# A long planned pause of TensorE takes several products with zeros instead of one

## Chip, cores, metric

The kernel runs on one core of a Trainium2 chip. The metric is the device time of one execution in microseconds (us). The core's engines are TensorE (PE; its weight loads are PEld), VectorE (DVE), ScalarE (ACT), GpSimd (POOL) and SyncE (SP, which issues the DMAs here). Every program is one launch, and the inputs are fixed.

## What is computed

Two pre-norm layers act on x of 8 sequences × 512 tokens × 128 features, all in float32:

```
x = x + linear_attention(layernorm(x))   # 16 heads × 64; elu(.)+1 features of q and k; sums over the sequence;
                                         # per feature q * kv / (q * ksum + eps); output projection; gelu
x = x + fp4_ffn(layernorm(x))            # inputs and weights rounded to blocks of FP4; 128 -> 352 -> 128, silu gate
x = x + causal_attention(layernorm(x))   # 16 heads × 8, softmax over a lower triangle
x = x + experts(layernorm(x))            # rms norm, 8 low-rank adapters on one shared 128 -> 512 -> 128 FFN,
                                         # the best 2 of 8 per token, weighted
```

## The kernel before, in words

Each sequence b (0 to 7) is one tile of 128 partitions × 4 × 128. It passes through eight kinds of work, the lanes: loads, norm, linear, out, fp4, attention, routing, experts. While one sequence is in its attention, others are in linear, fp4 or experts, so that the first 200 us are mostly linear and fp4 work, the middle has all of them, and the end has only the experts of the last sequence.

The kernel text doesn't issue instructions in the order in which it is written. It records steps: each call through `nc.<engine>` becomes a `Step` with its engine, its needs (steps that must be done) and a planned cost from a formula in `cost`. `Plan.ordered` (line 249) then plays the steps through with these costs and with a rank for each step from the table `TURNS`, and so gives every step a planned start and end and the program order of each engine. `Plan.issue` (line 397) writes the instructions in that order. On the chip each engine takes its own instructions strictly in program order and waits on semaphores for the others; the planned times play no part any more. Because all calls come out of `issue`, the profile shows nearly everything under one line, L407, and groups are told apart by the names of their tiles.

The names that the later sections use: `ahead` (one bank of PSUM), `pair` (two) and `mid` (one) are where products land. `wq`, `wk`, `wv` and `xnT` are the projections of the linear attention; each product of 512 columns is followed by `relu` and `exp` on ACT and a combination on DVE (`kf`, `qf`), then `z` (ACT), `r` (POOL, then the DVE reciprocals of some 1.7 us) and `qf` (POOL). `wk_o` is the weighted output matrix; four products of it make half of the linear attention's output, which goes to `y`. `xf`, `qa`, `sc`, `h`, `hq`, `wT` belong to fp4, `qkT`, `pr`, `va` and `mask_q` to the causal attention. `tT`, `a_sb`, `w_sb`, `um`, `b_sb`, `act` belong to the experts; `ohr`, `top`, `s4 routing` and `pb` to the routing. A float32 product of 512 columns appears in the profile as two MATMUL records.

`Plan.kept_warm` (line 365) runs over the finished order. For each step of TensorE it looks at the planned pause before it (`gap`) and at the work that TensorE had in the last 3.413 us of the plan (`worked`). Where work is lacking and `want` is over 0.2 us, it puts one extra step on TensorE's queue at the start of the pause: a product of up to 512 columns, `plan.warmer(n)` (line 907), whose moving operand is the tile `zeros` and whose weights are the identity, accumulated into `mid`. It adds zero to what is there. Its planned cost is 1.7 ns per column. In the profile these are the records `mid<-zeros,ident`; here they are called warmers. A warmer is left out where the planned time lies between TensorE's last write of `mid` and the last read of it (`read`), so that a reader of `mid` doesn't wait for it. Since the class `Clock` is not in use for durations (`MODEL` is false), the plan reckons with one speed of TensorE.

## Time and profile before

| | |
|---|---|
| time, median of 3 runs | 1132.38 us (1130.52 to 1133.14) |
| the profiled execution's own time | 1131.95 us |
| its span, first to last instruction | 1130.1 us |
| mean granted clock of TensorE | 0.982 |
| PE busy | 1040.2 us, 92% of the span |
| DVE / ACT / POOL busy | 73% / 56% / 55% |
| records of `mid<-zeros,ident` | 88 |

The span is 1.85 us shorter than the execution's time. Busy time of PE counts records that overlap by their modelled ends, so its share says where PE has work, and not how well it is used. In the rows of the timeline the first number is the start, the second the duration of a merged group, `xN` the number of its records, and the bracket the idle time of the engine before it with what ended it. In a windows view the pairs are busy time and number of records of each engine, then the mean granted clock, the share of the DMA engines and their GB/s. "Half clock" below is a granted clock of 0.50.

### The profile page before, as it was taken

To read this page: it belongs to the slowest core of one execution; us is meant where nothing else is said; L and a number is where in the kernel's file an instruction comes from. 1 tells how busy PE (TensorE), PEld (TensorE's weight loads), DVE (VectorE), ACT (ScalarE), POOL (GpSimd) and SP (SyncE) were. 2 spreads that over 40 slices of the span, in tenths; PEclk is the share of its full clock that TensorE was granted. 3 is DMA by queue.
4 is the path that set the end of the run, shared out by engine and by line. 5 is a ranking of instruction groups with operands and counts; after the bars stand their busy time and mean duration, and the time that the engine had idled before them with its cause. 6 is when DMAs were issued, how large, how long until landed. Compare 5 with 4: busy or idle time off the path is not lost.

```text
span 1130.1 us, 15043 instructions
## 1 busy us (share of the span) xinstructions
PE 1040.2 (92%) x5025; PEld 488.0 (43%) x5025; DVE 830.3 (73%) x1868; ACT 630.8 (56%) x1084; POOL 624.3 (55%) x669
## 2 busy tenths in 40 slices
PE   6667788998899999999998999999999999999998
PEld 2223333344344444444543444454454445445454
DVE  6868879897888967758788968788667765556543
ACT  5756787678786644644578555764443443344311
POOL 6647846676676466237635755467644533441534
PEclk9879989999999999999999999999999999999999
DMA  8000030001101020111012000210002102001000
GB/s 235 1 1 0 1 111 1 21 20 56 39 20 30 10 94 20 58 72 35 26 39 94 19 21 20 95 30 19 20 7 98 39 20 104 21 20 30 1 10 9
DMA packets 30572, 44.31 MB, mean 39 GB/s; under 512 B 4192, under 2 KB 18464, under 8 KB 30496
## 3 DMA queue, kind: packets, MB, share of 16 engines
q1 hardware_dynamic: 30496, 43.37, 11.9%
q8 instruction: 39, 0.64, 0.2%
q14 instruction: 37, 0.30, 0.1%
HBM read 23.95 MB, written 18.87 MB: 38 GB/s over the span
## 4 chain that ended last, share of the span: by engine, by line
PE 57%; DVE 15%; ACT 6%; issue 2%; POOL 1%; DMA 0%; POOLq 0%; DVEq 0%; ACTq 0%
PE ahead L407 31%; PE pair L407 19%; PE mid L407 7%; ACT pr L407 2%; DVE r L407 2%; DVE mx L407 2%; DVE h L407 1%; DVE sc L407 1%; ACT qf L407 1%; DVE s4 routing L407 1%; DVE qf L407 1%; DVE act L407 1%; ACT z L407 1%; DVE kf L407 1%; DVE oh L407 1%
## 5 line engine op out<-in xcount | busy, mean ns | idle before, releaser
L407 ACT ACTIVATE pr<-pair 128x1024 f32<-128x1024 f32 (+1 forms) x192 | 166.7, 879 | 149.2 <-PE pair L407 129.1
L407 DVE TENSOR_REDUCE mx<-pair 128x4 f32<-128x512 f32 (+2 forms) x192 | 198.5, 1041 | 68.4 <-PE pair L407 57.7
L407 POOL TENSOR_SCALAR_AFFINE_SELECT pr<-pr 128x256 f32<-128x256 f32 (+1 forms) x192 | 92.8, 485 | 176.4 <-ACT pr L407 175.6
L407 PE MATMUL pair<-qkT 32*128 32x128 f32 (+7 forms) x1024 | 172.3, 387 | 9.4 <-ACT pr L407 2.7
L407 PEld LDWEIGHTS pair<-qkT 32*128 32x128 f32 (+1 forms) x1024 | 84.4, 183 | 181.8 <-ACT pr L407 52.0
L407 POOL TENSOR_TENSOR act<-act,tw 128x512 f32<-128x512 f32 x64 | 81.3, 1272 | 88.8 <-DVE act L407 80.6
L407 PE MATMUL ahead<-um,b_sb 128*128 128x512 f32 x240 | 122.2, 607 | 0.0
L407 DVE RECIPROCAL r<-r 128x256 f32<-128x256 f32 x64 | 110.3, 1736 | 14.9 <-POOL r L407 14.8
L407 DVE SCALAR_TENSOR_TENSOR act<-act,ahead 128x512 f32<-128x512 f32 x120 | 81.9, 684 | 51.4 <-ACT act L407 38.0
L407 POOL TENSOR_TENSOR qa<-qa,qa 128x704 f32<-128x704 f32 (+4 forms) x60 | 81.2, 1354 | 35.1 <-DVE qa L407 26.2
L407 POOL TENSOR_TENSOR qf<-qf,r 128x512 f32<-128x512 f32 x64 | 80.5, 1278 | 34.5 <-DVE r L407 27.8
L407 PE MATMUL mid<-pr,va 128*10 128x512 f32 (+3 forms) x1024 | 93.3, 435 | 0.0
L407 POOL TENSOR_TENSOR qf<-qf,z 128x512 f32<-128x512 f32 x64 | 80.3, 1270 | 0.0
L407 ACT ACTIVATE act<-ahead 128x512 f32<-128x512 f32 x60 | 35.8, 597 | 72.0 <-PE ahead L407 71.9
L407 PE MATMUL ahead<-act,a_sb 128*128 128x512 f32 x128 | 65.2, 619 | 0.0
L407 POOL TENSOR_TENSOR r<-z,z 128x512 f32<-128x512 f32 x32 | 40.9, 1278 | 41.6 <-ACT z L407 39.3
L407 PE MATMUL ahead<-tT,w_sb 128*128 128x512 f32 x120 | 63.3, 609 | 0.0
L407 ACT ACTIVATE ahead<-ahead,bqkv_sb 128x512 f32<-128x512 f32 x96 | 63.0, 656 | 0.0
L407 PE MATMUL pair<-mask_q,ident 128*128 128x128 bf16 (+1 forms) x384 | 61.6, 242 | 0.0
L407 PE MATMUL ahead<-xnT,wk 128*128 128x512 f32 x100 | 56.7, 650 | 4.8 <-DVE kf L407 2.1
L407 PEld LDWEIGHTS ahead<-um,b_sb 128*128 128x128 f32 x240 | 40.7, 190 | 36.1 <-issue 29.6
L407 ACT ACTIVATE z<-qf,eps_sb,s 128x512 f32<-128x512 f32 x64 | 51.9, 811 | 6.8 <-DVE s L407 5.1
(227 smaller groups left out, 1986.4 us busy)
## 6 DMA issues: line engine op xcount, KB each, us to landing
stacks<-qk SPq DMA_DIRECT2D x32, 512.0 KB
qkT<-stacks SPq DMA_DIRECT2D x128, 128.0 KB
x<-in SPq DMA_DIRECT2D x8, 256.0 KB
qkT<-mr SPq DMA_DIRECT2D x128, 4.0 KB
out<-x SPq DMA_DIRECT2D x8, 256.0 KB
w_sb<-in SPq DMA_DIRECT2D x3, 256.0 KB
wq<-in SPq DMA_DIRECT2D x4, 128.0 KB
wk<-in SPq DMA_DIRECT2D x4, 128.0 KB
```

The source lines that it names most:

```text
L407: getattr(e, method)(*a, **k)
```

## The change

In `kept_warm`, a planned pause over 1.5 us now asks for warmers for at least 0.8 of its length, whatever TensorE did before it. And where one warmer of at most 512 columns doesn't use up what is wanted, another follows behind it in the same pause, until 0.2 us or less is left or the guard on `mid` says no. Warmers that are placed count as work for the pauses behind them. Nothing else is changed: the order of the real steps, their engines and their buffers are the same.

```diff
                 want = min(gap, TARGET * Clock.WINDOW - worked)
-                if want > 0.2 and not any(a - 0.5 < last < b + 0.1 for a, b in read):
+
+                if gap > 1.5:
+                    want = max(want, 0.8 * gap)
+                while want > 0.2 and not any(a - 0.5 < last < b + 0.1 for a, b in read):
                     n = min(512, 64 * int(want / 1.7e-3 / 64))
                     f = Step(-1, "tensor", None)
                     f.calls, f.cost, f.work = self.warmer(n), n * 1.7e-3, n * 1.67e-3
                     f.start, f.end = last, last + f.cost
                     past.append((f.start, f.end, 1.0))
                     out.append(f)
+                    last, want = f.end, want - f.cost
                 last = s.end
```

`TARGET` is 0.6 and `Clock.WINDOW` 3.413 us.

## The prediction

> **What bounds the kernel now.** I read the page first, for where TensorE (PE) is full and where its clock is cut:

> ```profile
> PE   6667788998899999999998999999999999999998
> PEclk9879989999999999999999999999999999999999
> ```

> Up to about 200 us PE is busy six to nine tenths and every cut of the clock but two lies there; later it is nearly full. The windows view by stage gives the same in numbers (us, then PE, PEld, DVE, ACT, POOL busy with counts, clock, DMA share, GB/s):

> ```profile
> 0.00:200.00 200.00, 150.29 (x396) 64.40 (x396) 155.31 (x397) 138.30 (x247) 125.24 (x145) 0.92 0.17 50
> ...
> 1084.00:1127.00 43.00, 41.98 (x158) 23.14 (x156) 17.04 (x28) 6.83 (x12) 17.56 (x14) 1.00 0.02 6
> ```

> So the question differs by stage: early, PE has idle time that a product with zeros (a warmer) can fill; at the end it has none. Next, what makes the clock fall: the same view, cut where the granted clock changes (stretches of 3.41 us).

> ```profile
> 61.91:65.32 3.41, 3.41 (x8) 1.85 (x8) 1.47 (x12) 1.86 (x6) 3.05 (x4) 0.50 0.03 5
> 96.04:99.45 3.41, 1.59 (x5) 0.55 (x5) 3.31 (x7) 1.02 (x2) 2.02 (x3) 1.00 0.00 0
> 113.11:116.52 3.41, 1.29 (x4) 0.39 (x3) 3.31 (x7) 1.81 (x4) 1.68 (x3) 1.00 0.00 0
> 116.52:119.93 3.41, 3.41 (x5) 1.30 (x4) 2.54 (x10) 1.99 (x4) 2.27 (x4) 0.50 0.00 0
> 137.00:140.41 3.41, 1.10 (x2) 0.30 (x2) 2.26 (x4) 1.42 (x4) 3.38 (x5) 1.00 0.00 0
> 143.83:147.24 3.41, 3.41 (x6) 1.35 (x5) 0.31 (x2) 3.33 (x8) 1.51 (x2) 0.50 0.00 0
> ```

> A stretch with 1.29 us of PE work is followed by half clock, one with 1.59 (1.02 of it a warmer, so zeros count as work) is not; a full stretch brings the clock back. Last, the timeline of PE at the two places that decide, start and end, and the chain of waits there:

> ```profile
> 3.84 2.08 PE L407 MATMUL mid<-zeros,ident 128*128 128x512 f32 x2 [3.84 <-POOL zeros L905]
> 8.38 1.62 PE L407 MATMUL ahead<-ident,xn 128*128 128x128 f32 x4 [2.46 <-ACT xn L407]
> ...
> 11.09 1.92 PE L407 MATMUL ahead<-xnT,wk 128*128 128x512 f32 x2
> ```

> ```profile
> 1112.50 1.02 PE L407 MATMUL mid<-zeros,ident 128*128 128x512 f32 x2
> 1113.36 7.03 PE L407 MATMUL ahead<-act,a_sb 128*128 128x512 f32 x16
> ...
> 1120.22 1.02 PE L407 MATMUL mid<-zeros,ident 128*128 128x512 f32 x2
> ...
> 1121.09 1.05 PE L407 MATMUL ahead<-w_sb,act 128*128 128x128 f32 x8
> ...
> 1122.51 0.49 PE L407 MATMUL ahead<-b_sb,um 128*128 128x128 f32 x2 [0.38 <-POOL um L407]
> ```

> ```profile
> 1091.22 0.65 PE mid L407 x2
> 1091.87 20.79 PE ahead L407 x48
> ```

> At the start real work waits 2.46 us behind the warmer; at the end each warmer is followed by the next product without a gap, and the warmer itself is a piece of the chain. The pauses that the planner saw there don't exist on the chip.

> **What is added.** The pauses are the planner's own, fixed by the kernel file; no time here is taken from them, only how many products the new rule places. Before, it places 44, and the trace has 88 records of them, two per product. Applied to its pauses, the rule gives (planned pause: columns before to after; start of the warmer in the trace; PE's idle time behind it):

> ```
>  8.30:  512-3904;  3.84; 2.46     1.91: 384- 896;  287.52; 1.10
>  3.36:  512-1536; 41.81; 0.45     1.64: 512- 768;  290.79; 1.63
> 10.47:  512-4864; 50.98; 9.29     1.75: 320- 768;  604.87; 0.80
>  4.49:  512-2048; 83.47; 1.19     1.89: 512- 832;  850.47; 1.91
>  2.06:  512- 960; 86.65; 1.97     1.50: 512- 704;  853.69; 0
>  2.24:  512-1024; 96.45; 1.82     1.85: 384- 832;  955.30; 0
>  2.88:  512-1344;113.01; 2.12     2.26: 512-1024; 1084.02; 0
>  3.48:  512-1536;135.34; 2.95     1.85: 384- 832; 1091.06; 0
>  3.18:  512-1472;165.29; 2.47     2.85: 512-1280; 1112.50; 0
>  1.59:  256- 704;171.46; 0        3.65: 512-1664; 1120.22; 0
> ```

> The loop also splits two shorter pauses (64 more columns at 339.80, 128 at 1070.80), and one warmer shrinks by 256 (at 294.40). Together 19,520 columns, 45 more products. Back to back, products of 512 columns start 0.86 us apart (22.16, 23.01, 23.87), at half clock 1.70 (11.09, 12.79): some 33 us of PE time. The load of its weights (190 ns a record, beside the running product) is in that spacing. A warmer waits for nothing but PE, issues no DMA, and is passed by no other queue; what queues behind it is PE's next product, and the engine that reads that product's result.

> **Covered at no cost.** From 41.81 to 165.29 an addition outgrows its room only at 41.81 (1.7 us against 0.45) and 83.47 (2.6 against 1.19). At 41.81 DVE is busy without a break from 37.88 to 53.2, so PE is early; the excess at 83.47 and the next addition (0.75) run into the 1.97 us before 89.64, and the next step of the chain, xf's second transposes at 90.94, is met. If that cover fails, 1.3 us each. At 287.52, 290.79, 604.87 and 850.47 the additions (0.86, 0.43, 0.75, 0.54) fit. At 1070.80 0.2 us goes into the 2.23 us before 1075.85.

> **Start.** 3904 columns are 7.6 products, 6.56 us at full clock. PE runs them from 3.84 at half clock until a whole stretch was busy: until 7.29 (stretches counted back from 116.52) or, with another position of the stretches, 10.67 at the latest. Half of that time is lost, so PE is free at 12.1 to 13.8, not before 8.38. Then transposes (0.60 in the warm row at 125.18), the copy (0.61) and the first K product at full clock (1.12 with its drain): its end, 13.00 before, moves to 14.5 to 16.2. The chain goes through it (ACT kf at 13.04, DVE kf at 14.31 after 3.20 idle), and DVE or ACT carries it to 61.29. Cost 1.5 to 3.2; I take 2.3.

> **Clock kept.** Three early stretches of half clock follow pauses that are now filled. After 50.98 the room is 9.29, the addition 7.3: the four wk_o products from 63.57 to 68.04 take 3.6 instead of 4.5 and the warmer ahead of them half; the transposes don't gain, as ACT's xn paces them: 1.4. After 113.01: wk, wv and four wk_o products, 116.15 to 123.27, shrink by 1.8; ACT had idled 1.47 before its next step, DVE 1.19 soon after: 1.0. After 135.34: 141.28 to 149.54 shrinks by 3.0, but xa and POOL's r for DVE at 147.03 come only 1.0 to 1.3 earlier: 1.2. At 850.47 the stretch rises from 1.50 us of work to about 2.0; the product behind 853.69 then starts 0.52 earlier in spite of 192 more columns and takes 0.86 instead of 1.72: gain 1.4, loss 0.6 (192 columns at half clock) if it falls nevertheless; I take 0.9. Bounds of the four: 0 to 9.1 together (1.4 + 1.8 + 3.0 + 1.4 and 1.5 more if the cut at 1075.66 goes too).

> [...]

> **Paid in full.** At 171.46 0.75 us, of which the next wait (0.46) takes most: 0.3. At 955.30 0.75, PE dense on both sides: 0.7. At 1084.02, 1091.06, 1112.50 and 1120.22: 0.86 + 0.75 + 1.29 + 1.93, less the 0.38 us wait for um at 1122.51, which then is over: 4.45. Nothing behind these is idle long enough to take it back.

> **Sum.** 2.3 − 1.4 − 1.0 − 1.2 − 0.9 + 0.3 + 0.7 + 4.45 = +3.25 us on the profiled execution's 1131.95 (span 1130.1 and 1.85 around it), which lies 0.43 under the median of 1132.38. Forecast 1135.4, between the two starting points (1135.2 and 1135.6).

> **Rivals.** (a) Faster: the clock is what early PE pays most for, and the chain follows it one for one. For it: PE is in the chain at 63.57, 116.15 and 141.28. Then 9.1 are gained, the start costs 0.7 (its waits of 1.03 at 20.94 and 0.58 at 28.39 take the rest of the 2.3), what is paid in full 5.45: −2.95, to 1129.0. It decides against my forecast if ACT and DVE really move up by 1.4, 1.8 and 3.0. Against it: their idle times there are shorter. (b) Slower still: nothing of the warmth reaches the chain, since DVE (155 of the first 200 us) ends each wait anyway; the start costs 3.2. Then 3.2 + 0.6 + 0.3 + 0.7 + 4.45 = +9.25, 1141.2. (c) No visible change: only the start is cheaper, by those two waits, 0.7 instead of 2.3: +1.65, 1133.6. The same could come of a change that places fewer products than the rule says; the count of 88 speaks against that.

> **How the numbers follow.** A measurement of this kernel tells 0.2% from no change, 2.3 us. My forecast 0.60 (its own range 1133 to 1138), (a) 0.16, (b) 0.14, (c) 0.10. Low end at (a), 1129.0; high end 1140, just short of (b). Faster: most of (a), 0.15. Same: (c), the low part of the forecast and the rest of (a): 0.28. Slower 0.57.

> **What would show it.** 178 records of mid<-zeros instead of 88, some 33 us of PE added; the first transposes of xn at 12 to 14; full clock from 7 to 11 on, and around 63, 118 and 143; no gap behind the last four warmers, and 4.45 us more than before from the warmer of 1084.02 to the end. The forecast is wrong if the tail doesn't lengthen by 4 to 5 us (then the end was not PE's), or if the early stage up to 200 us ends more than 3 us away from where it ends now.

## The result, and the profile after

The changed kernel takes 1135.3 us (median of 10 runs, 1131.76 to 1137.84); the kernel before, beside it, 1132.18 (10 runs, 1130.52 to 1133.28). The ratio is 1.0027, with a 95% interval of 1.0014 to 1.0040: slower by 3.1 us, just over what the measurement can tell. The profiled execution took 1136.38, its span 1134.5.

The page of after, PE busy and clock in 40 slices:

```profile
PE   7788888998899999999998999999999999999998
PEclk9989999999999999999999999999999999999999
```

PE is fuller in the first 200 us, and the cuts of the clock after about 85 us are gone from the digits. The windows view by stage (columns as before):

```profile
0.00:200.00 200.00, 166.42 (x456) 73.37 (x456) 154.94 (x396) 138.00 (x247) 125.23 (x145) 0.97 0.17 50
1084.00:1131.00 47.00, 46.79 (x174) 25.79 (x172) 17.00 (x28) 6.83 (x12) 17.59 (x14) 1.00 0.02 6
```

In the first 200 us PE has 16 us more to do, at a clock of 0.97 where it was 0.92; DVE, ACT and POOL have the same work as before. The last part, full before, has 16 more records and is longer. The group of the warmers, from the tile's view (records, shortest/median/longest in ns, first and last start):

```profile
L411 PE MATMUL mid<-zeros,ident x178: 217/591/1219, 3.8 to 1126.1; 128*128 128x512 f32 x108, 128*128 128x320 f32 x16, 128*128 128x256 f32 x16, 128*128 128x192 f32 x12
```

178 records, as worked out: the change does what its text says. PE's timeline at the start and at the end:

```profile
3.84 9.15 PE L411 MATMUL mid<-zeros,ident 128*128 128x512 f32 x16 [3.84 <-POOL zeros L909]
12.83 0.60 PE L411 MATMUL ahead<-ident,xn 128*128 128x128 f32 x4
13.27 0.81 PE L411 MATMUL mid<-zeros,ident 128*128 128x384 f32 x2
14.11 1.12 PE L411 MATMUL ahead<-xnT,wk 128*128 128x512 f32 x2
```

```profile
1114.35 2.32 PE L411 MATMUL mid<-zeros,ident 128*128 128x512 f32 x6
1116.50 7.03 PE L411 MATMUL ahead<-act,a_sb 128*128 128x512 f32 x16
1123.37 2.96 PE L411 MATMUL mid<-zeros,ident 128*128 128x512 f32 x8
1126.16 1.05 PE L411 MATMUL ahead<-w_sb,act 128*128 128x128 f32 x8
1127.06 0.39 PE L411 MATMUL ahead<-b_sb,um 128*128 128x128 f32 x2
```

At the start xn's transposes (`xn` is the normed input, transposed ahead of the K product `xnT,wk`) now begin at 12.83, behind the zeros and with no idle time, instead of at 8.38. At the end nothing separates warmer and product, and the wait for um is gone. The chain of waits there consists of PE alone:

```profile
1092.32 1.40 PE mid L411 x4
1093.72 20.79 PE ahead L411 x48
1114.51 2.15 PE mid L411 x6
1116.66 6.87 PE ahead L411 x16
1123.53 2.80 PE mid L411 x8
1126.33 4.48 PE ahead L411 x40
```

The 20.79 us of real products are as long as they were; the warmers around them have grown.

**Where the time went.** DVE executes the same 1868 instructions in the same order in both kernels. The difference of their starts, after minus before, grows where time is lost and falls where it is gained. A second profiled execution of the changed kernel (1131.80 us, from the experiments) stands in the last column:

| up to about (us) | shift, 1136.38 | shift, 1131.80 |
|---|---|---|
| 14, first K product | +2.23 | +1.71 |
| 36 | +1.55 | +1.03 |
| 68 | +1.42 | −0.37 |
| 126 | +0.75 | −1.31 |
| 152 | +0.40 | −2.82 |
| 203 | +0.45 | −4.18 |
| 857 | −0.87 | −5.46 |
| 958 | −0.11 | −4.69 |
| 1083 | +0.23 | −4.34 |
| 1124 | +4.44 | −0.13 |

Two things are in this table. From 857 us on both columns take the same steps, to 0.02 us: +0.77 at 955, +0.34 around 1070, and +4.21 over the last four pauses. And the two executions of one kernel differ by 4.6 us, all of it from before 203 us. There the stretches of half clock differ. In the traces of before and after, all records of the granted clock but the last, which ends with the trace, last whole multiples of 3.41 us: in before 20.48 us at 1.00 up to 34.60, then 6.83 at 0.50, 13.65 at 1.00 and 10.24 at 0.50; in after the longest is 873.82 us (256 × 3.413) at 1.00, from 203.13. A stretch is one such 3.41 us (below, a stretch that falls is one that runs at half clock). The runs without a trace point the same way: the ten of the changed kernel stand in the order of their mean granted clock, from 1131.76 us at 0.995 to 1137.84 at 0.989. Between 14 us and the end, the profiled execution of before has about 41 us of half clock (from 34.6, 55.1, 79.0, 116.5, 140.4, 198.4, 853.8 and 1075.7), that of after 17.1 (63.2, 80.3, 141.7, 199.7, 1076.9), the second one 10.2 (38.2, 79.2, 1072.5).

### The profile page after: what moved, and what is told of

Read it like the earlier page. It is cut to its first block, busy times and chain, and to the rows that moved or that the text cites. A ratio compares the mean times of both kernels' runs of the same rounds, so it can differ in the third digit from the quotient of the medians.

```text
span 1134.5 us, 15223 instructions
## 1 busy us (share of the span) xinstructions
PE 1063.5 (94%) x5115; PEld 501.4 (44%) x5115; DVE 831.1 (73%) x1868; ACT 630.4 (56%) x1084; POOL 624.3 (55%) x669
## 4 chain that ended last, share of the span: by engine, by line
PE 58%; DVE 15%; ACT 6%; issue 2%; POOL 1%; DMA 0%; DVEq 0%; ACTq 0%; POOLq 0%
PE ahead L411 31%; PE pair L411 19%; PE mid L411 8%; ACT pr L411 2%; DVE r L411 2%; DVE mx L411 2%; DVE h L411 1%; DVE sc L411 1%; ACT qf L411 1%; DVE s4 routing L411 1%; DVE qf L411 1%; DVE act L411 1%; ACT z L411 1%; DVE kf L411 1%; DVE oh L411 1%
## 5 line engine op out<-in xcount | busy, mean ns | idle before, releaser
L411 DVE TENSOR_REDUCE mx<-pair 128x4 f32<-128x512 f32 (+2 forms) x192 | 198.4, 1040 | 68.6 <-PE pair L411 57.8
L411 POOL TENSOR_TENSOR qf<-qf,z 128x512 f32<-128x512 f32 x64 | 80.3, 1270 | 0.0
L411 PE MATMUL mid<-zeros,ident 128*128 128x512 f32 (+7 forms) x178 | 72.5, 531 | 3.8 <-POOL zeros L909 3.8
L411 PE MATMUL ahead<-xnT,wk 128*128 128x512 f32 x100 | 54.3, 625 | 3.4 <-ACT xnT L411 1.7
```

Of the source, the lines that this page charges most:

```text
L411: getattr(e, method)(*a, **k)
```

## The experiments

Each kernel was timed beside the kernel before on the same chip, in three groups of runs; absolute times of different groups are not compared, only their ratios to the kernel before. In the diffs `last` is the planned time of the pause. Theory A is the sum of the prediction: the early products gain what the clock loses less, and the loss is the start and the late products. Theory B puts the loss into the early part behind the start and takes the late products for nearly free. In the last group the two differ on the price of the start alone. C, in two places, says that the late warmers of the kernel before hold the clock there.

**The first pause as before**, all the rest as in the change:

```diff
-                if gap > 1.5:
+                more = last > 1.0
+                if more and gap > 1.5:
                     want = max(want, 0.8 * gap)
...
                     last, want = f.end, want - f.cost
+                    if not more:
+                        break
```

> The change everywhere but in the first planned pause (8.3 us), which keeps its one warmer. Theory A (each stage's shift goes through to the end): the first xn transposes start at 8.4 again and the time is about 2.2 us under that of the change, some 1133.1. Rival B (the early stage absorbs a late start in its idle time, so that the end alone decides): within 0.5 us of the change, some 1135.3.

1135.13 us (12 runs), ratio 1.0027 [1.0006, 1.0047]; before 1131.78 (35 runs). That is the ratio of the whole change: taking its first pause back gave nothing, B's number. But the profile (1136.27) doesn't say that the start is free. Its shift is 0 at 14 us, where the change has +2.23; then two stretches fall to half clock that kept it in the change (28.7 and 158.4), the shift is +1.2 at 33 us, and from 161 us on the two executions agree to 0.15 us. In this execution the 2.2 us were saved and lost again. Nine runs lie at 1134.2 to 1136.3 (clock 0.986 to 0.992) and three at 1129.7 to 1130.2 (0.994 to 0.995): runs of one kernel lie further apart than the edit moves them, and the slower ones have the lower clock.

**Only the late pauses** (`more = last > 930.0`, otherwise the same edit):

> The change only in pauses whose planned start is over 930 us: 832 columns at 955, 640 at 1070, 1024, 832, 1280 and 1664 in the last four. Theory A: 0.75 + 0.86 + 0.75 + 1.29 + 1.5 = 5.1 us over the kernel before, some 1137.3, with nothing given back. Rival B (the late products come back out of later waits, and the loss of the change is its start): within 1 us of the kernel before, some 1132.5.

1136.52 (12 runs), ratio 1.0043 [1.0023, 1.0064]: 4.7 us over before. A said +5.1, B about nothing. In the profile the shift goes from +0.43 at 1083 us to +4.64 at 1124 us: +4.21 once more. The late products are paid in full.

**Only the early pauses** (`more = last < 200.0`):

> The change only in pauses whose planned start is under 200 us, the first included. Theory A: the start's +2.2 and the clock's gains up to 200 us (0.4 to 1.8 in one profile) nearly cancel: +0.5 us, some 1132.6, and no half clock at about 118 and 64. Rival B: the start is the loss, +2.5 to +4 us, 1134.7 to 1136.2.

1130.1 (12 runs), ratio 0.9995 [0.9976, 1.0014]. B's 1134.7 to 1136.2 is excluded; A's 1132.6 is nearer. The early part gains or loses nothing that this measurement can tell. Its profile starts later too (+2.81 at 14 us), has it back by 152 us and ends at −2.06.

**Before, without any late warmer**:

```diff
                 want = min(gap, TARGET * Clock.WINDOW - worked)
+                if last > 920.0:
+                    want = 0.0
```

> The kernel before, without any warmer whose planned pause ends after 920 us (ten of the 44). Theory A (a warmer in a dense stage is paid like any product): 0.86 + 0.65 + 0.2 + 0.5 + 0.86 + 0.65 + 0.86 = 4.6 us under the kernel before, some 1127.6; nothing from the one at 1120, since POOL's um ends that wait anyway. Rival C (they hold the clock there): half-clock stretches of 3.41 us appear between 940 and 1120, each worth up to 1.7 us, and the time is the same or higher.

1136.06 (12 runs), ratio 1.0050 [1.0028, 1.0071]. A expected a gain of 4.6 us and was wrong by over 8; C's half clock appears, in one place. Of the ten warmers that this removes, it is the two that the kernel before has at 1024.07 and 1025.70 that hold the clock. The windows view of this kernel, three of its stretches of 3.41 us:

```profile
1020.02:1023.43 3.41, 2.11 (x18) 1.08 (x22) 3.13 (x13) 2.39 (x3) 1.08 (x2) 1.00 0.27 76
1023.43:1026.85 3.42, 3.42 (x17) 1.08 (x18) 1.52 (x5) 1.77 (x3) 0.46 (x2) 0.50 0.01 2
...
1037.09:1040.50 3.41, 3.06 (x12) 0.68 (x10) 2.15 (x4) 0.54 (x2) 0.00 (x0) 0.50 0.01 2
```

After a stretch with 2.11 us of PE work the clock falls, and it stays at half for five stretches, though PE shows work for nearly all of them. The records overlap by their modelled ends: products of 512 columns are 1.02 us long and start 0.86 apart. An estimate that takes this overlap of 0.16 us off each record leaves 0.82 to 0.92 of each stretch busy. The kernel before has its two warmers in the next row and keeps the clock:

```profile
1023.43:1026.85 3.42, 3.19 (x18) 1.51 (x19) 2.62 (x13) 1.42 (x3) 0.10 (x1) 1.00 0.27 79
```

DVE's shift against before goes from −4.84 at 1028 us to +1.86 at 1040: 6.7 us lost there, more than the other eight warmers cost. This is one profile (1132.19 us, one of the fastest of the twelve), but all twelve runs have a clock of 0.968 to 0.978, under every one of the 35 of before (0.980 to 0.989).

**The change up to 900 us only** (`more = last < 900.0`; late pauses as before), and **the change once more** beside it:

> The change in all pauses with a planned start under 900 us; the six places of the last third as before. Theory A (the loss of the change is the products in the dense last third, 4.7 us when added alone): 4.5 to 5 us under the change, that is 1130 to 1131, under the kernel before by 1 to 3 us, as the early part alone was, with no half clock at about 854. Rival B (early and late parts are linked by the place of the clock's stretches, and the sum isn't additive): not under the kernel before.

> The changed kernel itself, beside the others and the kernel before on one chip. Both theories: 3 to 4 us over the kernel before, median 1135 to 1136; it serves as the base for the differences.

1129.28 (12 runs), ratio 0.9985 [0.997, 1.000], and 1134.56 (12 runs), ratio 1.0023 [1.0010, 1.0036]; before 1131.38 (23 runs). The repeat confirms the loss. The difference of the two, 5.28 us, is the price of the products that the change adds behind 900 us; the shifts give 0.76 + 0.34 + 4.21 = 5.31 for the same (that the two agree so closely is luck, as both kernels spread over 5 to 7 us). A said 4.5 to 5 us, and that early and late parts add up is against B. Whether the change up to 900 us is under the kernel before, as A said, is not told by an interval that ends at 1.000.

The repeat also shows how one kernel differs from itself: of its 12 runs five lie at 1131.8 to 1132.5 (clock 0.994 to 0.995) and seven at 1134.4 to 1137.0 (0.989 to 0.992). The windows view of its profiled execution (1131.80), two stretches around 62 us (their place counted on from its half clock at 38.24, seven times 3.41 to 62.13):

```profile
58.72:62.13 3.41, 1.61 (x5) 0.57 (x3) 3.41 (x7) 0.35 (x1) 2.31 (x3) 1.00 0.00 0
62.13:65.55 3.42, 3.06 (x10) 1.72 (x11) 1.48 (x13) 1.88 (x5) 3.15 (x3) 1.00 0.00 0
```

And the slower execution of the same kernel at the same place:

```profile
59.77:63.19 3.42, 1.42 (x5) 0.52 (x3) 3.42 (x12) 0.89 (x3) 2.32 (x3) 1.00 0.00 0
63.19:66.60 3.41, 3.37 (x7) 1.98 (x8) 1.49 (x12) 1.87 (x5) 3.06 (x4) 0.50 0.00 0
```

The same gap of 1.99 us lies between the last warmer and xn's transposes in both. In the slower one a stretch begins and ends so that it holds 1.42 us of PE work, and the next runs at half clock; in the faster one the stretches end 1.06 us earlier (62.13 instead of 63.19) and the work comes 0.53 earlier, so that the stretch holds 1.61, and the clock stays. The step of the shift from 36 to 68 us is −1.40 in one and −0.13 in the other.

**The change up to 900 us, without the warmers of the dense part**, the two at 1024 and one at 1069 kept:

```diff
                     want = max(want, 0.8 * gap)
+                if 920.0 < last < 1000.0 or last > 1065.0:
+                    want = 0.0
```

> The change up to 900 us, and none of the warmers at 942, 955, 994, 1084, 1091, 1112 and 1120 (all followed by PE without a gap); those at 1024, 1026 and 1070 stay. Theory A (a warmer in a dense stage is paid like any product; only the two at 1024 hold the clock): 0.86 + 0.65 + 0.2 + 0.86 + 0.65 + 0.86 = 4.1 us under the version with the change up to 900, some 1126.5. Rival C (each late warmer holds the clock, as the run without any of them was slower): half-clock stretches appear between 940 and 1120 and the time is no lower.

1126.82 (6 runs), ratio 0.9956 [0.9939, 0.9973]: faster than both kernels. The median is the one A gave, but A's step was 4.1 us under the version with the change up to 900, and the medians have 2.5 (1129.28 to 1126.82). By the shift between the two profiles it is 4.3 us from 900 us to the end, about 1 of it from a stretch that was at half clock at 1072.3 and is not any more; the warmer at 942 cost nothing. No half clock appears between 940 and 1120 us, against C. PE's timeline at its end:

```profile
1108.28 7.03 PE L416 MATMUL ahead<-act,a_sb 128*128 128x512 f32 x16
1115.15 1.20 PE L416 MATMUL ahead<-w_sb,act 128*128 128x128 f32 x8
1117.43 0.49 PE L416 MATMUL ahead<-b_sb,um 128*128 128x128 f32 x2 [1.08 <-POOL um L416]
```

Without a warmer ahead of the last products the wait for um is 1.08 us. So the single warmer of before was free there (taking it out moved the shift by 0.01 us); it is the three more behind it that cost.

**Before, without any warmer** (`want = 0.0` everywhere):

> The kernel before without any warmer. Theory A: in the early stage the chain pays for some more half-clock stretches (each 0.3 to 1.3 us on the chain), at 1024 five stretches as in the run without late warmers (6 to 7 us), less 4.6 us of late products: 1134 to 1142. Rival (warmers buy nothing, they only occupy PE): 1127 or less. A granted clock well under 0.978 goes with theory A.

1144.3 (5 runs), ratio 1.0127 [1.0106, 1.0149]; clock 0.958. The 44 warmers of before are worth 13 us, somewhat more than the 1134 to 1142 that A gave and against the rival. The shift is +6.8 at 203 us, +4.5 comes around 299 to 382 us, and here too stretches in a row run at half clock, four of them, from 1035 us.

**The first pause with one, with two products, the base again, and whole pauses.** All four are the change up to 900 us without the dense warmers, three of them with one edit more. The first pause gets one product or two:

```diff
+                if last < 1.0:
+                    want = 0.88      # the other kernel: 1.75
```

The fourth fills pauses whole instead of to 0.8:

```diff
-                    want = max(want, 0.8 * gap)
+                    want = max(want, (0.8 if last < 1.0 else 1.0) * gap)
```

> The version with the change up to 900 us and no warmers in the dense places, but with one product of 512 columns in the first pause, as before. Theory A (the start's delay of 1.6 to 2.8 us, seen at 14 us in every profile with the long fill, goes through to the end): 1.7 to 2.2 us under that version run beside it. Rival B (the earlier full clock pays the delay back by 160 us, as the run with the old start suggested): within 0.7 us of it.

> The same with two products in the first pause: at half clock they fill 3.84 to 7.3, so the first transposes are on time at 8.4, and the clock is full from between 7.3 and 10.7 on instead of 11 to 15. Theory A: 2 to 2.5 us under the version run beside it, a little better than one product. Rival B: within 0.7 us of it.

> The version with the change up to 900 us and no warmers in the dense places, again, as the base of this call: 1126.5 to 1127 in its median by both theories, 4.5 us under the kernel before.

> The same base with 1.0 instead of 0.8 of each long planned pause from the second on. If the 2.0 us left idle before 62.85 in the changed kernel's profile are why that stretch lost the clock, no half clock comes at 59 to 66 any more, worth 1.4 us in those executions that had it, about half of them; against it stand 0.2 of the other pauses: 84 and 171 us are already full and pay 0.9 and 0.3 us more. Sum: within 1 us of the base. The other theory (the chain there doesn't follow PE) expects the same time without any gain at 62 to 68.

| | median (runs) | range | ratio to before |
|---|---|---|---|
| base again | 1127.15 (10) | 1122.90 to 1128.38 | 0.9960 [0.9945, 0.9975] |
| one product | 1122.21 (6) | 1120.92 to 1123.42 | 0.9923 [0.9905, 0.9941] |
| two products | 1120.63 (6) | 1119.88 to 1124.97 | 0.9917 [0.9898, 0.9936] |
| pauses whole | 1124.51 (5) | 1124.43 to 1125.68 | 0.9948 [0.9931, 0.9964] |

Before was 1131.48 (15 runs). The base repeats its ratio. A short first pause gains 4.9 to 6.5 us, far more than A's 1.7 to 2.5 and than B's 0.7; none of the theories has it. Profiles settle a part of it. The base has two: one at 1126.85 (the run before this group) with half clock from 63.0, 80.1, 141.5 and 199.5 us, and one at 1122.90 with half clock from 38.1, 79.1 and 140.5. By DVE's shift they are 4.0 us apart, all of it before 204 us. The profile with two products (1124.97, the slowest of its six) has its half clock where the base's slower one has it (61.3, 78.3, 139.8, 197.8): it is 2.13 us ahead at 20 us and 1.88 ahead at the end. So where the same stretches fall, the delay of the start goes through, as A said. The profile with one product (1122.42) has a pattern like the faster base, with one stretch more (34.2 to 41.0): of its 1.65 us ahead 0.48 are left at the end. What the medians differ by beyond 1.9 us would then be that most runs of the base have the slower pattern and most with a short start the faster one. That is argued, not shown: the runs without a trace have only their mean clock, and it overlaps (0.990 to 0.995 in the base, 0.993 to 0.997 with one or two products). With two products the transposes start when xn is there, as in before:

```profile
3.85 3.78 PE L418 MATMUL mid<-zeros,ident 128*128 128x512 f32 x4 [3.85 <-POOL zeros L916]
8.39 1.63 PE L418 MATMUL ahead<-ident,xn 128*128 128x128 f32 x4 [0.76 <-ACT xn L418]
```

It has the lowest median of all that was run, 0.8% under the kernel before; from the one product it is not told apart. With pauses filled whole, the gap at 60 us is gone and no stretch near it falls; three of its five runs have a clock of 0.998, at 1124.4 to 1124.5. Its median is 2.6 us under the base, more than the 1 us expected, but the intervals of the ratios overlap: unclear.

## Why the prediction was right, and where its steps were not

The forecast was 1135.4 and the time is 1135.3, with the sign as foretold. The agreement to 0.1 us is luck, and better than the steps deserve: it holds for the median of a kernel whose runs spread over 6 us. Of the two profiled executions one ended 4.4 us over the one of before and the other 0.15 under it, where +3.25 was summed.

**Paid in full, 5.45.** Right, and tested: +4.21 from 1084.02 to the end in each of three profiles where 4.45 was summed, +0.77 at 955.30 where 0.7 was, and 5.28 us when all late additions were taken back. The first two of the four pauses cost 0.86 and 0.76 as summed, the third 1.29, the last 1.30 instead of 1.55 (1.93 − 0.38): the wait for um at 1122.51 swallowed 0.25 us more than its idle time of 0.38 showed. The step counted as free, 1070.80, cost 0.34, of which 0.21 are there by 1074 us, ahead of the half clock that follows. The prediction let its 0.2 us of zeros go into PE's wait before 1075.85; but PE's product of `act,a_sb` came later by them, POOL's `act` behind it started later (after 1.07 us of idle time instead of 0.85), and DVE's `oh` beside that took 1.12 us instead of 0.92.

**Covered at no cost.** Right in both profiles: no lasting step of the shift comes at 41.81, 83.47, 287.52, 290.79 or 604.87.

**Start, 2.3.** Right as a local price: +2.23 and +1.71 at the first K product, 1.6 to 2.8 in seven profiles with the long fill, and the transposes at 12.83. The trace records full clock from 8.57 us on, that of before from 14.12. What it costs at the end depends on what falls behind it. Where the same stretches fall, 1.88 of 2.13 us went through. Taken back inside the change it gave nothing (ratio 1.0027 both times), and the profile shows two other stretches falling instead; taken back in the base of the last group it gave 4.9 us. So it is no plain term of a sum: it also shifts everything after it against the stretches. Five to twelve executions of each kernel and one or two profiles don't settle how often which pattern comes.

**Clock kept, 4.5 in four places.** Here the working failed as a method, and not only in size. In the profiled execution the steps are −0.13, −0.67, −0.35 and −1.32, in the other −1.40, −0.94, −1.51 and −1.28, where −1.4, −1.0, −1.2 and −0.9 were predicted. The faster execution confirms the mechanism nearly everywhere, the slower one for two of four. The 0.3 us at 171.46 is seen in neither. After 50.98 the prediction took it for granted that a fill of 7.3 of 9.29 us keeps the clock; the remaining 2 us are enough to lose it, if they fall into one stretch. After 135.34 likewise:

```profile
138.28:141.69 3.41, 1.47 (x3) 0.30 (x2) 2.19 (x4) 0.68 (x2) 3.38 (x5) 1.00 0.00 0
141.69:145.11 3.42, 3.09 (x5) 1.81 (x6) 2.87 (x12) 0.98 (x2) 0.38 (x1) 0.50 0.00 0
```

After a stretch with 1.47 us of work the clock falls; at 116.52 and 851.66, after 2.68 and 2.04 us, it stays:

```profile
116.52:119.93 3.41, 2.68 (x8) 1.08 (x7) 3.27 (x13) 1.60 (x3) 2.50 (x2) 1.00 0.00 0
...
851.66:855.07 3.41, 2.04 (x9) 0.87 (x8) 2.27 (x5) 0.67 (x2) 2.59 (x2) 1.00 0.72 250
```

And two stretches that the prediction passed over moved the time as well: at 34.6 (−0.68 in both) and at 198.4 (−1.36 in the second alone). The prediction's own sign, full clock around 63, 118 and 143 us, came true in the second execution alone; the first has half clock at 63.2 and 141.7. Filling short idle times did pay: behind the warmers at 113.01, 135.34 and 850.47 PE stood idle for 2.12, 2.95 and 1.91 us in before, half clock followed (from 116.52, 140.41 and 853.80), and the steps there are 2.34 us together in one execution and 3.73 in the other. After 50.98 the 1.99 us left idle were enough to lose the clock in the first.

Two things misled the working. It read 1.59 us of work in a stretch as enough; in the same profile of before the stretch at 195.03 with 1.76 us is followed by half clock (lines in the last section). And it read the positions of half clock from one execution of before as if they belonged to the kernel. The two executions of this kernel show that they don't: the instructions are the same, the stretches end 1.06 us apart (62.13 and 63.19), and the times differ by 4.6 us. That is 0.4% of 1132 us, but more than this change's whole effect of 3.1 us.

By the prediction's own tests: the tail lengthened by 4.21, inside the 4 to 5. The early stage up to 200 us moved by +0.45 in one execution and by −4.18 in the other, which is over the 3 us allowed. So the forecast of the early stage holds for the first and fails for the second.

**The rivals.** (a) wanted 9.1 us of gain; the most is 7.2, from +1.71 to −5.46 in the second execution, part of it at places that (a) didn't have. (b) is excluded by the early pauses alone, which cost nothing, and by the time. (c)'s +1.65 lies at the lower end of what was measured (+1.6 to +4.5), so the time alone hardly excludes it; but its two waits at 20.94 and 28.39 took nothing of the late start, as the shift is still +2.24 just before 36 us.

## What to carry to other kernels

A filler product was worth its time here only where the engine really stood still on the chip and the clock fell (as after the 2.12 us of idle time behind 113.01); in the dense stage it was one more link of the chain, at its full duration (+4.21 us over the last four pauses), and a planner's pause there was no evidence of a real one. So give the dense part no filler at all unless its removal is shown to lose the clock, fill real pauses only up to where the next product is ready, and test removals one place at a time: here seven late warmers cost 2.5 us together by the medians (4.3 by the profiles), and two others were worth 6.7.

Where the clock is decided by stretches that lie differently in each execution (here 1.06 us apart in two), read the half-clock places from several profiles before summing them, and give such a term the width of their difference.

## What the runs showed of the hardware that was not expected

```profile
195.03:198.44 3.41, 1.76 (x6) 0.67 (x5) 3.24 (x4) 2.81 (x6) 1.82 (x2) 1.00 0.00 1
198.44:201.86 3.42, 3.42 (x6) 1.01 (x5) 2.05 (x7) 1.97 (x3) 2.31 (x3) 0.50 0.00 0
```

```profile
191.84:195.25 3.41, 1.76 (x7) 0.62 (x5) 3.24 (x5) 3.09 (x6) 1.38 (x2) 1.00 0.01 2
195.25:198.67 3.42, 3.33 (x10) 1.16 (x8) 2.49 (x7) 2.52 (x3) 2.31 (x3) 1.00 0.00 0
```

- With more work than that the clock stayed, but for five stretches with products of the attention: the one with 2.11 us at 1020.02, three in the kernel without any warmer (2.10 to 2.71), and one with 3.42 at 693.43 where pauses were filled whole. Many of those products have 32 or 34 rows of weights instead of 128, and they are short (386 ns in the mean for `pair<-qkT` on the page of after, 607 for `ahead<-um,b_sb`), so that modelled ends count for more (with 0.16 us off each, the estimate from above, the 2.11 are some 1.5). That the rows are the reason wasn't tested.
- Half clock outlasted nearly full stretches: five in a row without late warmers (1023.43 to 1040.50 us), with an estimated 0.82 to 0.92 of PE work, and four without any (from 1035 us). In the kernel before, with its two warmers at 1024.07 and 1025.70, the stretch at 1023.43 stayed at 1.00.
- The run times of one kernel fall into groups that are some 4 to 6 us apart: in the first group of experiments the kernel before had 11 of 35 runs at 1125.9 to 1127.1 (clock 0.985 to 0.989), and the others at 1130.5 to 1133.9 (0.980 to 0.985).
